# A two-layer convolution and attention kernel: the softmax sum's last step on VectorE, edge and overlap copies on ScalarE, and other places for the first value tiles of an image

## The chip, the core and the metric

The kernel runs on one NeuronCore of one Trainium2 chip. The metric is the device time of one execution in microseconds (us), lower is better. Five engines work side by side, each through its own list of instructions in order: TensorE (PE in the profile), VectorE (DVE), ScalarE (ACT), GpSimd (POOL) and SyncE (SP). SP does no arithmetic here; it issues nearly all DMA transfers.

## What is computed

The input is x, eight images of 256 channels and 64 x 64 pixels in float32. Two layers follow, each as x + layer(groupnorm(x)). Cut to what matters:

```python
# layer 0: per-pixel 3x3 weights made from the image, applied to x3
x1, x2, x3 = conv1x1(x, w1, b1), conv1x1(x, w2, b2), conv1x1(x, w3, b3)   # 32, 32, 256 channels
x2u = unfold3(pad(x2, 1, mode='reflect'))
h = relu(bn1(concat([x1, x2u])));  h = relu(bn2(conv1x1(h, cw1)));  w = conv1x1(h, cw2, cb2)
out = einsum('bgskhw,bgkhw->bgshw', unfold3(zero_pad(x3)), w)

# layer 1: 7x7 local attention with 4 heads, plus a dynamic 3x3 branch
q, k, v = conv1x1(x, Wq) * HD**-0.5, conv1x1(x, Wk), conv1x1(x, Wv)
att = softmax(einsum('bdn,bdkn->bnk', q, unfold7(reflect_pad3(k)) + unfold7(reflect_pad3(pe))))
out_att = einsum('bnk,bdkn->bdn', att, unfold7(reflect_pad3(v)))
wts = softmax(einsum('oc,bchw->bohw', Wfc, x).reshape(b, C, 9, h, w), axis=2)
oc = dwconv(relu(dwconv(x, w1)), w2)                       # depthwise 3x3 twice
out = rate1 * out_att + rate2 * sum(oc * wts, over the 9)
```

## The kernel before, in words

**Bands and steps.** An image is cut into NB = 8 bands of R = 8 rows, so there are 64 bands, written here as (image, band). The main loop goes over the bands g; g starts at -12, and bands below zero are a prologue that does layer 0 alone. In each band the loop makes eight steps s: two halves of the channels (ct = 0, 1; 128 channels each) by four pairs of 8 x 8 pixel tiles (m). Layer 1 of band g runs together with layer 0 of band g + 12, so from (6,4) on there is no layer 0 left to do, and bands get shorter.

**The order is written by hand.** There is no planner. A step is a fixed sequence of calls with six `advance()` calls between them, called places here. `after(n, f)` puts f n places later, and `advance()` runs what is due. `beside(g, s)` returns two lists of calls for a step: `mid` runs in the middle of the step, `end` at its end. What is called first stands first in its engine's list, and an engine that waits holds up all that stands behind it.

**What a step puts on TensorE.** Scores of two tile pairs (`scores`, L737, at even steps, from the keys `kb` and the queries `qb`), the weighted values of the two pairs before (`weighted_values`, L786, from the value tiles `vt`), the transposes of probabilities (L774), two weight maps of the dynamic branch (`branch_weights`, L873), and besides, spread over the steps, queries (L672), keys (L693), values (L592) and the layer-0 matmuls (L328, L369, L430, L466). Results that leave through the PSUM tag `gen` share four buffers, so a matmul into a fifth waits until the oldest has been read.

**Layer 0, small maps.** At step 0 `small_maps` runs L328, and `write_maps` has ScalarE write three shifted copies of x2 and the map x1 into a tile of 10 rows (eight ACTIVATEs, L343 and L347). Then the left and right border columns and the border rows are filled by copies on GpSimd (L351 to L360); a row is also handed to the band before.

**Layer 0, products.** Nine times a band VectorE multiplies a tap weight with shifted x3 (`prod`, L479, two buffers) and GpSimd adds it up (`xg`, L487). x3 comes back from DRAM as `x3q` (L389 to L397).

**Keys.** `queries` makes a new key tile `kb` of 14 rows by 70 columns and copies the six rows that it shares with the band before on GpSimd (L668). `keys` runs L693; its `finish` has VectorE add bias and position (L701) and, for the three reflected columns on either side, do the same again from PSUM (L708, three instructions a piece). In the first and the last band of an image the reflected rows follow on ScalarE (L718), and keys and queries are placed one step earlier.

**Values.** `values` (two halves) computes a band of values, and ScalarE copies it into `vc` (L600; one buffer). `store_values` writes it to a DRAM tile `vd` with its reflected columns (L616 to L625). `value_tile` loads the four tiles `vt` (L642) that the attention reads. An inner band takes 8 loads. The first key band of an image (j = 0) and the last (j = 8) have three mirrored rows; there each mirrored row is loaded by itself, which makes 32 loads. For the next image's first two bands, values are made during band 7 of the current image at steps 4 and 5 (j = 0) and 6 and 7 (j = 1); the tiles of j = 0 are loaded at the end of step 7, those of j = 1 at the ends of steps 0, 1 and 2 of the new image's first band.

**The dynamic branch's softmax.** ScalarE takes the exponentials (L878), GpSimd adds pairs up (L1080). `dynamic_sum` then adds the two halves (L886), adds 1 and limits the sum to 1e37 in one instruction (L889), both on GpSimd; VectorE takes the reciprocal in two halves (L894, placed 9 and 13 places on), and GpSimd multiplies and adds to the result `xr` (L895, L899, L900), which SP stores (L905). For the very last sum of the kernel all of it is on VectorE.

Of the kernel before, what the change touches and what calls it, by code (L numbers as in the profile page):

```python
# [13 lines left out]
ALU = mybir.AluOpType  # L14
# [9 lines left out]
R = 8  # L24
BAND = R * W
NB = H // R
# [21 lines left out]
PAD = KA // 2  # L48
WP = W + 2 * PAD
TQ = 8  # L50
# [3 lines left out]
KW = TQ + 2 * PAD  # L54
# [32 lines left out]
def conv_layers_kernel(ctx: ExitStack, tc: tile.TileContext, ins: dict, out: bass.AP):  # L87
    nc = tc.nc
# [121 lines left out]
    images = [Image() for b in range(B)]  # L210
# [4 lines left out]
    def after(n, f):  # L215
        later.append((place[0] + n, f))
# [118 lines left out]
    def write_maps(b, i, p12):  # L335
        im = images[b]
        t = im.x2[i] = w0.tile([P, HR, W], F32, tag="x2", name=f"x2_{b}_{i}", bufs=2)
        bias = im.bias
        for u in range(2):
            r, o = u * R // 2, 64 * u  # L340
            for q, (dst, src) in enumerate(((1, 0), (0, 0), (0, 1))):
                n = W - (q != 1)
                nc.scalar.activation(  # L343
                    t[32 * q : 32 * q + 32, r + 1 : r + 1 + R // 2, dst : dst + n],
                    p12[o : o + 32, :, src : src + n], AF.Identity, bias=bias[o : o + 32, 0:1],
                )
            nc.scalar.activation(  # L347
                t[96:128, r : r + R // 2, :], p12[o + 32 : o + 64], AF.Identity, bias=bias[o + 32 : o + 64, 0:1]
            )

        nc.gpsimd.tensor_copy(t[0:32, 1 : 1 + R, 0:1], t[0:32, 1 : 1 + R, 2:3])  # L351
        nc.gpsimd.tensor_copy(t[64:96, 1 : 1 + R, W - 1 : W], t[64:96, 1 : 1 + R, W - 3 : W - 2])

        if i == 0:
            nc.gpsimd.tensor_copy(t[0:96, 0, :], t[0:96, 2, :])
        else:
            nc.gpsimd.tensor_copy(t[0:96, 0, :], im.x2[i - 1][0:96, R, :])
            nc.gpsimd.tensor_copy(im.x2[i - 1][0:96, R + 1, :], t[0:96, 1, :])
        if i == NB - 1:
            nc.gpsimd.tensor_copy(t[0:96, R + 1, :], t[0:96, R - 1, :])  # L360

    def value_maps(b, i, mt):

# [200 lines left out]
    def strided(v, at, *dims):  # L564

        return bass.AP(v.tensor, v.offset + at, [v.ap[0], *dims])
# [40 lines left out]
    def store_values(b, j):  # L607
# [9 lines left out]
        for d in range(1, PAD + 1):  # L617
            for to, c in ((PAD - d, d), (PAD + W - 1 + d, W - 1 - d)):
# [3 lines left out]
                else:  # L622
                    for p in range(2):
                        o = vd[at + p : at + p + 2 * count[p] - 1 : 2, to : to + 1].rearrange("u c n -> c u n")
                        nc.sync.dma_start(out=o, in_=vc[p * W + c : p * W + c + 1, : count[p]])  # L625

    def value_tile(b, j, u):


        im = images[b]  # L630
        vd = im.vd[j]
        vt = im.vt[j, u] = w1.tile([CHUNK, 2, C], F32, tag="vt", name=f"vt_{b}_{j}_{u}", bufs=11)
        if j == 0:
            runs = [(PAD, PAD, R - PAD)] + [(PAD - d, PAD + d, 1) for d in range(1, PAD + 1)]
        elif j < NB:
            runs = [(0, 0, R)]
        else:
            runs = [(0, 1, PAD)] + [(PAD - 1 + d, PAD - d, 1) for d in range(1, PAD + 1)]
        for to, at, n in runs:
            for g in range(2):  # L640
                c0 = (2 * u + g) * TQ
                nc.sync.dma_start(  # L642
                    out=vt[to * KW : (to + n) * KW, g], in_=vd[at : at + n, c0 : c0 + KW]
                )

    def new_keys(i):

# [14 lines left out]
    def queries(b, i, ct):  # L662

        im = images[b]
        nm = f"{b}_{i}_{ct}"
        kb = im.kb[i, ct] = w1.tile([P, KW, WP], F32, tag="kb", name=f"kb_{nm}", bufs=3)
        if i:
            nc.gpsimd.tensor_copy(kb[:, : 2 * PAD], im.kb[i - 1, ct][:, R:])  # L668
        qb = im.qb[i, ct] = w1.tile([P, NT, TQ, TQ], F32, tag="qb", name=f"qb_{nm}")
        pq = ps.tile([P, R, W], F32, tag="gen", name=f"pq_{nm}", bufs=4)  # L670
        for kt in range(NCT):
            nc.tensor.matmul(  # L672
                pq, wq[:, kt, ct * P : (ct + 1) * P], im.yp[i][:, kt, PAD : PAD + R],
                start=(kt == 0), stop=(kt == NCT - 1),
            )
        nc.scalar.activation(
            qb.rearrange("p t r c -> p r t c"), pq.rearrange("p r (t c) -> p r t c", c=TQ),
            AF.Identity, bias=bq[:, ct : ct + 1], scale=HD**-0.5,
        )

    def keys(b, i, ct):


        im = images[b]
        first, last = new_keys(i)
        kb, pe = im.kb[i, ct], im.pe[i]
        bk = chan[:, ct, CBK : CBK + 1]
        pieces = []
        for a in range(first, last, R):
            n = min(R, last - a)  # L690
            pk = ps.tile([P, R, W], F32, tag="gen", name=f"pk_{b}_{i}_{ct}_{a}", bufs=4)
            for kt in range(NCT):
                nc.tensor.matmul(  # L693
                    pk[:, :n], wk[:, kt, ct * P : (ct + 1) * P], im.yp[i][:, kt, a : a + n],
                    start=(kt == 0), stop=(kt == NCT - 1),
                )
            pieces.append((a, n, pk))

        def finish():
            for a, n, pk in pieces:  # L700
                nc.vector.scalar_tensor_tensor(  # L701
                    kb[:, a : a + n, PAD : PAD + W], pk[:, :n], bk, pe[:, a - first : a - first + n],
                    ALU.add, ALU.add,
                )

                for d in range(1, PAD + 1):
                    src = (W, n), (W - 1 - 2 * d, 2)
                    nc.vector.scalar_tensor_tensor(  # L708
                        strided(kb, a * WP + PAD - d, (WP, n), (W - 1 + 2 * d, 2)), strided(pk, d, *src), bk,
                        strided(pe, (a - first) * W + d, *src), ALU.add, ALU.add,  # L710
                    )
            if i in (0, NB - 1):
                after(2, reflect)

        def reflect():
            for d in range(1, PAD + 1):
                to, at = (PAD - d, PAD + d) if i == 0 else (last - 1 + d, last - 1 - d)
                nc.scalar.copy(kb[:, to], kb[:, at])  # L718

        return finish  # L720
# [159 lines left out]
    def dynamic_sum(b, i, ct, ex, oc):  # L880

        tot = w1.tile([P, BAND], F32, tag="tots", name=f"tot_{b}_{i}_{ct}", bufs=1)
        xr = images[b].xr[i]

        engine = nc.vector if (b, i, ct) == (B - 1, NB - 1, NCT - 1) else nc.gpsimd
        engine.tensor_add(tot, ex[:, 1], ex[:, 0])  # L886


        engine.tensor_scalar(tot, tot, 1.0, 1.0e37, ALU.add, ALU.min)  # L889
        rec = w1.tile([P, BAND // 2], F32, tag="rec", name=f"rec_{b}_{i}_{ct}", bufs=1)  # L890

# [12 lines left out]
        def store():  # L904
            nc.sync.dma_start(  # L905
                out=out[b].rearrange("(t p) n -> p t n", p=P)[:, :, i * BAND : (i + 1) * BAND], in_=xr
            )

        after(9, lambda: quotient(0))
        after(13, lambda: quotient(1))  # L910
        after(15, weigh)


    def beside(g, s):

        b, i = divmod(g, NB)
        bn, inx = divmod(g + 1, NB)
        mid, end = [], []
# [15 lines left out]

        made = [(b, i + 2, 4)] if g >= 0 and i < NB - 1 else []
        if i == NB - 1 and 0 <= b + 1 < B:
            made = [(b + 1, 0, 4), (b + 1, 1, 6)]
        for bb, j, d in made:
            if s in (d, d + 1) and (j < NB or s == d):
                mid.append(lambda bb=bb, j=j, d=d: values(bb, j, s - d))  # L940
            if s == d + 1:
                end.append(lambda bb=bb, j=j: store_values(bb, j))
            if s == 7 and d == 4:
                for u in range(NT // 2):
                    end.append(lambda bb=bb, j=j, u=u: value_tile(bb, j, u))
        if g >= 0 and i == 0 and s in (0, 1, 2):
            for u in {0: (0,), 1: (1,), 2: (2, 3)}[s]:
                end.append(lambda u=u: value_tile(b, 1, u))

        nxt = [(b, i + 2, 0)] if g >= 0 and i + 2 < NB else []  # L950
        if i == NB - 1 and 0 <= b + 1 < B:
# [25 lines left out]
        if 0 <= g + AHEAD - 2 < B * NB and s in TAPS_AT[g < -1]:  # L977
            u = TAPS_AT[g < -1].index(s)
# [28 lines left out]
    with tc.manual_schedule():  # L1007

        for i, use in enumerate(("xc", "xc", "xr", "xr", "xs", None, None, None)):
            t = None  # L1010
            if use is None:
                t = w1.tile([P, NCT, RP, W], F32, tag="yp", name=f"x_{i}", bufs=3)
                t = t.rearrange("p t r c -> p t (r c)")[:, :, :BAND]
# [15 lines left out]
        for g in range(-AHEAD, B * NB):  # L1029
            b, i = divmod(g, NB)  # L1030
            for s in range(STEPS):
                ct, m = divmod(s, NT // 2)
                mid, end = beside(g, s)
                steer(g, s)
                if g >= 0:
# [17 lines left out]
                    tot = exponentials(nm, prob, nmax)  # L1053
# [128 lines left out]
```

## Time and profile before

| what | value |
|---|---|
| median of 3 runs | 4016.24 us (4015.74 to 4016.27) |
| the profiled execution's own time | 4010.67 us |
| its span in the trace | 4008.9 us |
| mean granted TensorE clock | 0.988 |
| busy share PE, DVE, POOL, ACT | 95%, 85%, 79%, 71% |
| DMA, mean over the span | 117 GB/s |
| loads of value tiles (L642) | 960 |

The page of the profile gives busy times of each engine, groups of instructions by source line, and the chain of work that ended last. The trace answers further views: the timeline of an engine, what an engine's idle time waited for, and busy times in stretches of time. A line of the timeline has the start in us, the busy time, the engine, the source line, the operation, the output and inputs, the shapes and the count; in brackets stands how long the engine sat idle before it and what ended that. A line of the stretches has for each engine its busy us and its number of instructions, then the granted clock and the DMA share. [...]

### The profile page before, as it was taken

To read this page: it belongs to the slowest core of one execution; us is meant where nothing else is said; L and a number is where in the kernel's file an instruction comes from. 1 tells how busy PE (TensorE), PEld (TensorE's weight loads), DVE (VectorE), ACT (ScalarE), POOL (GpSimd) and SP (SyncE) were. 2 spreads that over 40 slices of the span, in tenths; PEclk is the share of its full clock that TensorE was granted. 3 is DMA by queue.
4 is the path that set the end of the run, shared out by engine and by line. 5 is a ranking of instruction groups with operands and counts; after the bars stand their busy time and mean duration, and the time that the engine had idled before them with its cause. 6 is when DMAs were issued, how large, how long until landed. Compare 5 with 4: busy or idle time off the path is not lost.

```text
span 4008.9 us, 72420 instructions
## 1 busy us (share of the span) xinstructions
PE 3807.0 (95%) x24620; PEld 2116.9 (53%) x24620; DVE 3419.8 (85%) x7143; ACT 2839.5 (71%) x6779; POOL 3174.8 (79%) x2156
## 2 busy tenths in 40 slices
PE   6879999999999999999999999999999999999998
PEld 3445555555555555555555555555555555555554
DVE  5868988888888988888988888978988889977888
ACT  3457777677676777777777677777777677676776
POOL 4758988788987988878887888978888888965665
PEclk9989999999999999999999999999999999999999
DMA  8864543544444443444443544444443544322220
GB/s 230 201 165 113 134 114 104 136 125 113 127 115 122 124 124 101 125 132 120 124 115 104 138 125 118 110 130 124 118 115 90 129 116 104 85 61 88 71 65 32
DMA packets 493171, 469.42 MB, mean 117 GB/s; under 512 B 68432, under 2 KB 394624, under 8 KB 492544
## 3 DMA queue, kind: packets, MB, share of 16 engines
q1 hardware_dynamic: 489472, 460.23, 43.4%
q10 hardware_dynamic: 3328, 4.55, 0.3%
q8 instruction: 195, 3.19, 0.3%
q14 instruction: 176, 1.44, 0.1%
HBM read 325.64 MB, written 138.99 MB: 116 GB/s over the span
## 4 chain that ended last, share of the span: by engine, by line
PE 27%; POOL 26%; DVE 22%; ACT 10%; issue 7%; DMA 5%; SPq 3%; POOLq 0%; DVEq 0%; ACTq 0%
PE pf L873 13%; POOL xg L487 13%; POOL ex L1080 6%; DVE prod L479 5%; DVE acc L856 5%; DVE rec L894 4%; PE small L786 3%; ACT x L343 3%; PE sco L737 2%; PE ptp L774 2%; ACT ex L878 2%; DVE prob L751 2%; DMA x3q<-x 2%; PE pq L672 2%; DVE acc L830 2%
## 5 line engine op out<-in xcount | busy, mean ns | idle before, releaser
L873 PE MATMUL pf<-yp,c_wfc 128*128 128x512 f32 x4096 | 1917.1, 597 | 6.2 <-ACT ex L878 5.1
L487 POOL TENSOR_TENSOR xg<-xg,prod 128x1024 f32<-128x1024 f32 x549 | 1200.7, 2187 | 177.2 <-DVE prod L479 148.3
L873 PEld LDWEIGHTS pf<-yp,c_wfc 128*128 128x128 f32 x4096 | 744.0, 191 | 730.3 <-issue 647.1
L1080 POOL TENSOR_TENSOR ex<-ex,ex 128x1024 f32<-128x1024 f32 x384 | 907.9, 2364 | 55.9 <-ACT ex L878 51.8
L479 DVE SCALAR_TENSOR_TENSOR prod<-pw,c_par,x3q 128x1040 f32<-128x1040 f32 x576 | 737.9, 1288 | 124.8 <-PE pw L466 56.1
L830 DVE SCALAR_TENSOR_TENSOR acc<-yp,c_chan,acc 128x504 f32<-128x504 f32 (+3 forms) x1104 | 775.0, 702 | 50.7 <-ACT acc L821 30.3
L856 DVE SCALAR_TENSOR_TENSOR acc<-hid,c_chan,acc 128x504 f32<-128x504 f32 (+3 forms) x1024 | 749.8, 732 | 18.1
L878 ACT ACTIVATE ex<-pf 128x512 f32<-128x512 f32 x1024 | 602.1, 588 | 204.2 <-PE pf L873 184.3
L759 ACT ACTIVATE prob<-prob,nmax 128x196 f32<-128x196 f32 x1024 | 459.2, 451 | 217.1 <-DVE nmax L751 216.9
L768 ACT ACTIVATE prob<-prob,tot 128x196 f32<-128x196 f32 x1024 | 413.0, 452 | 235.3 <-DVE tot L766 235.1
L895 POOL TENSOR_TENSOR tot<-tot,rec 128x256 f32<-128x256 f32 x254 | 185.4, 730 | 412.9 <-DVE rec L894 387.9
L894 DVE RECIPROCAL rec<-tot 128x256 f32<-128x256 f32 x256 | 445.9, 1742 | 17.2 <-POOL tot L889 12.3
L776 ACT COPY pt<-ptp 112x512 f32<-112x512 f32 x511 | 294.8, 577 | 123.4 <-PE ptp L774 122.3
L751 DVE CUSTOM_DVE_ANT_0 prob<-sco,c_mask 128x196 f32<-128x196 f32 x1024 | 324.5, 354 | 20.4 <-PE sco L737 20.2
L786 PE MATMUL small<-pt,vt 112*64 112x64 f32 x8144 | 300.3, 226 | 37.5 <-DMA vt<-vd 37.1
L774 PEld LDWEIGHTS ptp<-ident,prob 128*112 128x112 f32 x2044 | 228.1, 134 | 188.9 <-issue 135.2
L774 PE MATMUL ptp<-ident,prob 128*112 128x128 f32 x2044 | 322.9, 281 | 1.3 <-ACT vc L600 1.3
L786 PEld LDWEIGHTS small<-pt,vt 112*64 112x64 f32 x8144 | 261.5, 138 | 116.7 <-issue 75.4
L737 PE MATMUL sco<-kb,qb 64*64 64x196 f32 x4096 | 236.1, 343 | 39.6 <-DVE kb L708 32.9
L592 PE MATMUL pv<-c_wv,yp 128*128 128x256 f32 (+1 forms) x1056 | 252.8, 382 | 2.6 <-ACT ex L878 2.1
L369 PE MATMUL p<-xc,w3s 128*128 128x512 f32 x512 | 248.4, 609 | 7.0 <-ACT ex L878 7.0
L466 PEld LDWEIGHTS pw<-h2n,c_c 128*128 128x128 f32 x1152 | 173.3, 191 | 153.5 <-issue 113.1
(139 smaller groups left out, 4756.9 us busy)
## 6 DMA issues: line engine op xcount, KB each, us to landing
vt<-vd SPq DMA_DIRECT2D x448, 112.0 KB
x<-x3n SPq DMA_DIRECT2D x128, 264.0 KB
x3q<-x SPq DMA_DIRECT2D x128, 264.0 KB
xc<-in_x SPq DMA_DIRECT2D x64, 512.0 KB
xg<-in_x SPq DMA_DIRECT2D x256, 128.0 KB
x<-xg SPq DMA_DIRECT2D x256, 128.0 KB
yp<-x SPq DMA_DIRECT2D x128, 256.0 KB
xr<-x SPq DMA_DIRECT2D x64, 512.0 KB
```

What stands on the lines that cost most here:

```text
L479: nc.vector.scalar_tensor_tensor(prod[:, :, :RUN], pw[:, j, :RUN].unsqueeze(1).to_broadcast([P, SHARE, RUN]), par[:, PCB2 + k : PCB2 + k + 1],
L487: nc.gpsimd.tensor_add(im.xg[i], im.xg[i], rows(prod))
L759: nc.scalar.activation(prob[:, h, :NKEY], prob[:, h, :NKEY], AF.Exp, bias=nmax[:, h : h + 1], scale=-1.0, accum_out=tot[:, h : h + 1],)
L768: nc.scalar.activation(prob[:, h, :NKEY], prob[:, h, :NKEY], AF.Copy, scale=tot[:, h : h + 1])
L774: nc.tensor.transpose(ptp[:, h, ch], prob[:, h, ch * CHUNK : (ch + 1) * CHUNK], ident)
L786: nc.tensor.matmul(po[half[h], :, t * TQ : (t + 1) * TQ], im.vt[i + ch, m][:n, t, (2 * ct + h) * HD : (2 * ct + h + 1) * HD], pt[:n, h, ch ...
L830: nc.vector.scalar_tensor_tensor(o, yp[:, ct, ra + dr : rb + dr, ca + dc : cb + dc], chan[:, ct, CW1 + k : CW1 + k + 1], o, ALU.mult, ALU.add,
L856: nc.vector.scalar_tensor_tensor(o, hid[:, ra + dr : rb + dr, ca + dc : cb + dc], chan[:, ct, CW2 + k : CW2 + k + 1], o, ALU.mult, ALU.add,)
L873: nc.tensor.matmul(pf, wfc[:, kt, 2 * m + j, ct * P : (ct + 1) * P], images[b].yp[i][:, kt, PAD : PAD + R], start=(kt == 0), stop=(kt == N ...
L878: nc.scalar.activation(ex[:, j].rearrange("p (r c) -> p r c", r=R), pf, AF.Exp)
L894: nc.vector.reciprocal(rec, v)
L1080: after(4, lambda ex=ex, exb=exb: nc.gpsimd.tensor_add(ex, ex, exb))
```

## The change

Four things are edited. (1) In `write_maps` the border copies go from GpSimd to ScalarE, and in `queries` the copy of the overlapping key rows does too. (2) In `keys` the reflected columns are no longer computed on VectorE from PSUM; one place later ScalarE copies them inside the key tile. (3) In `dynamic_sum` the "add 1, limit" instruction moves from GpSimd to VectorE and is placed 7 places later. (4) For j = 0 and j = 8 the mirrored rows are written once in DRAM (`mirror_rows`, three DMAs from `vd` to `vd`, one step after the values were stored), so that every value tile takes 2 loads and a band 8; the next image's first values are made one step earlier (steps 3 and 4, and 5 and 6), and the tiles of j = 1 are loaded in the middle of steps 0 and 2.

```diff
@@ write_maps
-        nc.gpsimd.tensor_copy(t[0:32, 1 : 1 + R, 0:1], t[0:32, 1 : 1 + R, 2:3])
-        nc.gpsimd.tensor_copy(t[64:96, 1 : 1 + R, W - 1 : W], t[64:96, 1 : 1 + R, W - 3 : W - 2])
+        nc.scalar.copy(t[0:32, 1 : 1 + R, 0:1], t[0:32, 1 : 1 + R, 2:3])
+        nc.scalar.copy(t[64:96, 1 : 1 + R, W - 1 : W], t[64:96, 1 : 1 + R, W - 3 : W - 2])
...
-            nc.gpsimd.tensor_copy(t[0:96, 0, :], im.x2[i - 1][0:96, R, :])
-            nc.gpsimd.tensor_copy(im.x2[i - 1][0:96, R + 1, :], t[0:96, 1, :])
+            nc.scalar.copy(t[0:96, 0, :], im.x2[i - 1][0:96, R, :])
+            nc.scalar.copy(im.x2[i - 1][0:96, R + 1, :], t[0:96, 1, :])
...
@@ values
+    def mirror_rows(b, j):
+        vd = images[b].vd[j]
+        for d in range(1, PAD + 1):
+            to, at = (PAD - d, PAD + d) if j == 0 else (PAD + d, PAD - d)
+            nc.sync.dma_start(out=vd[to], in_=vd[at])
@@ value_tile
-        if j == 0:
-            runs = [(PAD, PAD, R - PAD)] + [(PAD - d, PAD + d, 1) for d in range(1, PAD + 1)]
-        elif j < NB:
-            runs = [(0, 0, R)]
-        else:
-            runs = [(0, 1, PAD)] + [(PAD - 1 + d, PAD - d, 1) for d in range(1, PAD + 1)]
-        for to, at, n in runs:
-            for g in range(2):
-                c0 = (2 * u + g) * TQ
-                nc.sync.dma_start(
-                    out=vt[to * KW : (to + n) * KW, g], in_=vd[at : at + n, c0 : c0 + KW]
-                )
+        at, n = (0, R) if j < NB else (1, 2 * PAD)
+        for g in range(2):
+            c0 = (2 * u + g) * TQ
+            nc.sync.dma_start(out=vt[: n * KW, g], in_=vd[at : at + n, c0 : c0 + KW])
@@ queries
-            nc.gpsimd.tensor_copy(kb[:, : 2 * PAD], im.kb[i - 1, ct][:, R:])
+            nc.scalar.copy(kb[:, : 2 * PAD], im.kb[i - 1, ct][:, R:])
@@ keys
-                for d in range(1, PAD + 1):
-                    src = (W, n), (W - 1 - 2 * d, 2)
-                    nc.vector.scalar_tensor_tensor(
-                        strided(kb, a * WP + PAD - d, (WP, n), (W - 1 + 2 * d, 2)), strided(pk, d, *src), bk,
-                        strided(pe, (a - first) * W + d, *src), ALU.add, ALU.add,
-                    )
+            after(1, columns)
...
+        def columns():
+            for a, n, _ in pieces:
+                for d in range(1, PAD + 1):
+                    nc.scalar.copy(
+                        strided(kb, a * WP + PAD - d, (WP, n), (W - 1 + 2 * d, 2)),
+                        strided(kb, a * WP + PAD + d, (WP, n), (W - 1 - 2 * d, 2)),
+                    )
@@ dynamic_sum
-        engine.tensor_scalar(tot, tot, 1.0, 1.0e37, ALU.add, ALU.min)
+        def limit():
+            nc.vector.tensor_scalar(tot, tot, 1.0, 1.0e37, ALU.add, ALU.min)
...
+        after(7, limit)
@@ beside
-            made = [(b + 1, 0, 4), (b + 1, 1, 6)]
+            made = [(b + 1, 0, 3), (b + 1, 1, 5)]
...
+            if s == d + 2 and j in (0, NB):
+                end.append(lambda bb=bb, j=j: mirror_rows(bb, j))
-            if s == 7 and d == 4:
+            if s == 7 and j != 1:
...
-        if g >= 0 and i == 0 and s in (0, 1, 2):
-            for u in {0: (0,), 1: (1,), 2: (2, 3)}[s]:
-                end.append(lambda u=u: value_tile(b, 1, u))
+        if g >= 0 and i == 0 and s in (0, 2):
+            for u in (s, s + 1):
+                mid.append(lambda u=u: value_tile(b, 1, u))
```

More of the change, by code (lines that the diff above doesn't have):

```diff
@@ L349, in write_maps @@
             )
-        nc.gpsimd.tensor_copy(t[0:32, 1 : 1 + R, 0:1], t[0:32, 1 : 1 + R, 2:3])
-        nc.gpsimd.tensor_copy(t[64:96, 1 : 1 + R, W - 1 : W], t[64:96, 1 : 1 + R, W - 3 : W - 2])
+        nc.scalar.copy(t[0:32, 1 : 1 + R, 0:1], t[0:32, 1 : 1 + R, 2:3])
+        nc.scalar.copy(t[64:96, 1 : 1 + R, W - 1 : W], t[64:96, 1 : 1 + R, W - 3 : W - 2])
         if i == 0:
-            nc.gpsimd.tensor_copy(t[0:96, 0, :], t[0:96, 2, :])
+            nc.scalar.copy(t[0:96, 0, :], t[0:96, 2, :])
         else:
-            nc.gpsimd.tensor_copy(t[0:96, 0, :], im.x2[i - 1][0:96, R, :])
-            nc.gpsimd.tensor_copy(im.x2[i - 1][0:96, R + 1, :], t[0:96, 1, :])
+            nc.scalar.copy(t[0:96, 0, :], im.x2[i - 1][0:96, R, :])
+            nc.scalar.copy(im.x2[i - 1][0:96, R + 1, :], t[0:96, 1, :])
         if i == NB - 1:
-            nc.gpsimd.tensor_copy(t[0:96, R + 1, :], t[0:96, R - 1, :])
+            nc.scalar.copy(t[0:96, R + 1, :], t[0:96, R - 1, :])
     def value_maps(b, i, mt):
```

## The prediction

> **What bounds the kernel now.** I read the page first, then TensorE's idle gaps band by band.
>
> ```profile
> PE 3807.0 (95%) x24620; PEld 2116.9 (53%) x24620; DVE 3419.8 (85%) x7143; ACT 2839.5 (71%) x6779; POOL 3174.8 (79%) x2156
> ```
>
> TensorE is the bound nearly everywhere, so an edit is worth only what it does to TensorE's gaps. The stretches of one band each show where they are: (6,0), (6,1), then (7,0), (7,1).
>
> ```profile
> 3147.20:3213.60 66.40, 61.44 (x383) 33.15 (x382) 53.60 (x119) 45.20 (x110) 47.38 (x33) 0.97 0.48 123
> 3213.60:3271.90 58.30, 57.49 (x379) 32.10 (x378) 50.98 (x105) 43.53 (x104) 50.46 (x35) 1.00 0.43 115
> 3597.50:3656.00 58.50, 52.71 (x325) 29.03 (x324) 41.52 (x105) 36.44 (x93) 29.90 (x20) 0.94 0.31 95
> 3656.00:3705.60 49.60, 49.60 (x321) 27.10 (x320) 39.64 (x93) 36.13 (x88) 30.43 (x21) 1.00 0.22 71
> ```
>
> An image's first band takes 8 to 9 us more than the next, though it has only 0.65 us more matmuls (3 more key rows). The timelines of SP, ACT and PE in (6,0) say why:
>
> ```profile
> 3142.50 16.92 SPq L642 DMA_DIRECT2D vt<-vd  x32
> ...
> 3165.55 1.44 SPq L642 DMA_DIRECT2D vt<-vd  x2
> 3167.11 0.40 SPq L553 DMA_DIRECT2D yp<-x  x1
> ```
>
> ```profile
> 3168.50 0.55 PE L786 MATMUL small<-pt,vt 112*64 112x64 f32 x8 [2.08 <-DMA vt<-vd]
> ```
>
> ```profile
> 3171.61 1.13 ACT L562 ACTIVATE yp<-yp,aff 128x896 f32<-128x896 f32 x1 [5.38 <-DMA yp<-x]
> ```
>
> SP needs 16.92 us to issue 32 loads for j = 0. What stands behind them, the tiles of j = 1 and the rows for the next band, comes late, and TensorE and ScalarE wait. Over the run TensorE waits 37.1 us for `vt`.
>
> An ordinary band, (2,2), has only small gaps. TensorE's timeline, ScalarE's and VectorE's:
>
> ```profile
> 1343.16 0.92 PE L737 MATMUL sco<-kb,qb 64*64 64x196 f32 x16 [0.75 <-DVE kb L708]
> ...
> 1354.09 1.98 PE L369 MATMUL p<-xc,w3s 128*128 128x512 f32 x4 [0.18 <-ACT ex L878]
> ...
> 1372.57 0.92 PE L737 MATMUL sco<-kb,qb 64*64 64x196 f32 x16 [0.17 <-DVE kb L708]
> ...
> 1401.55 0.92 PE L737 MATMUL sco<-kb,qb 64*64 64x196 f32 x16 [0.76 <-DVE kb L708]
> ```
>
> ```profile
> 1352.95 0.47 ACT L347 ACTIVATE x<-small,bias 32x256 f32<-32x256 f32 x1
> 1353.44 0.60 ACT L878 ACTIVATE ex<-pf 128x512 f32<-128x512 f32 x1
> ```
>
> ```profile
> 1355.66 0.17 DVE L766 RECIPROCAL tot<-tot 128x2 f32<-128x2 f32 x1 [2.73 <-ACT prob L759]
> ...
> 1389.96 1.30 DVE L479 SCALAR_TENSOR_TENSOR prod<-pw,c_par,x3q 128x1040 f32<-128x1040 f32 x1 [0.53 <-POOL xg L487]
> ...
> 1400.23 0.73 DVE L701 SCALAR_TENSOR_TENSOR kb<-pk,c_chan,pe 128x512 f32<-128x512 f32 x1
> 1400.88 0.52 DVE L708 SCALAR_TENSOR_TENSOR kb<-pk,c_chan,pe 128x16 f32<-128x16 f32 x3
> ```
>
> The three places that stop TensorE (1354.09, 1372.57, 1401.55; call them P1, S4, S0) hang on ScalarE's block of `write_maps` and on VectorE's keys. TensorE has no slack to hide a delay there.
>
> [...] The trace agrees for full partitions (L818, 128x128: 289 ns, the next one 0.19 us later), but L343 and L347 on 32 partitions follow each other at 0.47 us, their full duration. [...] after the 5.78 us gap in (7,0) the granted clock of the band is 0.94.
>
> **The change part by part.**
>
> *Border copies on ScalarE.* Four copies a band (two of 32x8, two of 96x64) stand between L347 at 1352.95 and the exponential at 1353.44, which frees the PSUM buffer that P1 waits for. [...] Taken: 0.7. P1's stall grows from 0.18 to 0.88, and all on ScalarE behind it, L759 of step 1 included, moves by 0.7. GpSimd loses 0.84 us a band.
>
> *Limit on VectorE.* L889 takes 1.92 us on GpSimd; its one run on VectorE took 0.43. It stands after L766 of step 1 (and of step 5), so VectorE's unbroken run from 1355.66 to S4's keys moves by 0.70 + 0.43 = 1.13. It newly waits for GpSimd's L886; that ends at 1349.93 for the first, and for the second, once L889 and the key copy are gone from GpSimd, by my count about 1 us before VectorE gets there. So no wait is added.
>
> *Reflected columns on ScalarE.* L708's 0.44 to 0.52 us leave VectorE; three copies of 128x16 follow on ScalarE[...]. Taken: 0.5. They stand behind L768, which waits for L766.
>
> *Key overlap on ScalarE.* 128x420, [...]twice a band. Behind L768 of steps 2 and 6, where ScalarE next idles 0.80 and 1.04 us for VectorE; cost nothing. [...]
>
> *An ordinary band, summed.* S4: L701 (1371.25 to 1371.98) ends 1.13 later, at 1373.11; L768's pair ends at 1372.08 + 1.13 = 1373.21; columns 0.5; the 0.15 from keys to scores as before: 1373.86 for 1372.57, **+1.29**. That delays the tap weights for which VectorE waits at 1381.43. From there to L701's end VectorE takes 19.53 us; its waits on GpSimd (0.53, and 0.16 before L894) go, since GpSimd is 2.5 us lighter in that stretch; the second limit adds 0.43: 19.27, so L701 ends at 1401.99. L768 ends 0.11 later, columns and hand-over 0.65: 1402.75 for 1401.55, **+1.20 us a band**. There are 33 such bands (bands 1 to 5 of images 0 to 5, and (6,1) to (6,3)): 40 us. Bands (b,6) of six images have S4 alone (the next keys come a step early): 8. Band 7 stalls 1.27 and up to 1.32 us on ScalarE already, after `write_maps` and at step 3; I put 1.9 on each of six: 11. (6,4) and (6,5): 1. From (6,6) on VectorE waits for TensorE: nothing. **Loss 60**; ends 42 (copies overlapped) to 78.
>
> *Value tiles.* 960 loads become 576 and 48 DRAM copies; at a first band SP issues 8 for 32, at 0.53 us each (16.92 / 32) 13 us sooner free. The copies wait for the stores of `vd` and hold SP up, some 2 us by estimate, two steps ahead of the loads; behind them are stores of x1 and a load of x that aren't urgent. In band 7, though, 14 stores (9 us) now precede x3q, which isn't wanted until step 1 of the next band, and ScalarE's next `vc` (one buffer) can wait about 3 us for them; four PSUM buffers cover TensorE. First bands of images 1 to 6 took 66.76, 69.43, 67.16, 68.81, 67.30, 66.36 (405.8). After: 57.3 of matmuls in (6,1) + 0.6 + 1.5 (the 0.79 stall at P1 plus 0.7) + 0.9 and 1.0 (the present ScalarE stalls at steps 4 and 6, grown by the limit) + 1.0 before the next S0 = 62.3, six times 373.8: 32 saved. (7,0): 58.5 to 50.3: 8. (0,0): 72.65, where the first 5.7 us run at half clock: to 65.2: 7.5. Prologue, values one step sooner: 3, between 0 and 8. **Gain 50.5**; ends 35 to 66.
>
> Net +9.5: 4020 for the profiled execution's 4010.67, which lies 5.6 below the median of the runs; **4026 us** on that scale. No change, as far as a measurement here can tell, is within 0.2%, 8 us.
>
> **Rivals.** *Faster (0.28).* The copies overlap[...]: a band grows by 0.9 (30 + 6 + 5 = 41), and the first bands reach 60.0 (gain 66): 3991. For it: L818's 0.19 us. Against: L347's 0.47. It decides below +0.9 us an ordinary band, a length of 59.3. *The limit waits for GpSimd (0.10).* If L886 ends 1 us later than VectorE arrives, all behind it waits, some 1 us in 33 bands: 4060. GpSimd's 5 us idle before L895 speak against. *The gain isn't had (0.12).* One `vc` buffer and the DRAM copies make new waits of image starts, half the gain goes: 4051. For it: ScalarE waited 11.87 us for `vd<-vc` before the first band. *As forecast (0.50)*, 4008 to 4045, of which 0.17 within 0.2%.
>
> **How the numbers follow.** Slower 0.33 + 0.10 + 0.12 = 0.55, same 0.17, faster 0.28. The ends combined give 4016 + 42 - 66 = 3992 and 4016 + 78 - 35 = 4059: range 3990 to 4060. The likeliest case alone: 4008 to 4045.
>
> **What would show it.** Right: band (2,2) at 59.6 us with P1's stall near 0.9, "sco" waiting for ACT in place of DVE; first bands near 62 with no wait on `vt`. Wrong: ordinary bands at 58.4 or below, or first bands above 65.

## The result, and the profile after

The changed kernel takes **4034.73 us** (median of 5 runs, 4029.57 to 4044.25) against 4016.27 for the kernel before (median of 5 runs beside it, 4015.74 to 4021.51): a ratio of 1.0046, 95% interval 1.0031 to 1.0061. It is slower by 18.5 us. The forecast was 4026 with a range of 3990 to 4060, and slower as the likeliest side. The execution profiled took 4035.98 us, its span is 4034.0.

Line numbers have moved by a few in the changed kernel: the scores L737 are here L739, the exponentials L878 are L880, the limit L889 is L892. The page's line of busy times, to be laid beside that of before:

```profile
PE 3802.1 (94%) x24620; PEld 2111.2 (52%) x24620; DVE 3449.8 (86%) x6838; ACT 2974.6 (74%) x7579; POOL 2836.0 (70%) x1661
```

GpSimd lost 339 us of work and ScalarE gained 135. VectorE has 305 instructions fewer and is yet busy 30 us longer, which is a first hint of what the prediction missed.

The stretches of one band each, as the prediction showed them for before: an ordinary band (2,2), then (6,0), (6,1) and (7,0). After the length come busy time and instructions of PE, weight loads, VectorE, ScalarE and GpSimd, then the granted clock.

```profile
1356.00:1416.00 60.00, 57.38 (x378) 31.97 (x378) 53.12 (x103) 45.33 (x116) 45.05 (x27) 1.00 0.47 120
3179.30:3241.20 61.90, 58.92 (x383) 32.42 (x382) 53.10 (x111) 46.51 (x123) 44.60 (x26) 1.00 0.55 140
3241.20:3301.30 60.10, 57.39 (x378) 31.96 (x378) 52.02 (x101) 45.40 (x117) 45.31 (x27) 1.00 0.43 112
3630.80:3681.10 50.30, 50.30 (x325) 27.75 (x324) 40.93 (x98) 37.94 (x104) 25.62 (x18) 1.00 0.34 106
```

Both halves of the forecast are there. The first bands fell from 66.4 to 61.9 and from 58.5 to 50.3 us, and an ordinary band rose from 58.3 to 60.1. SP's timeline in (6,0) has the gain: the mirrored rows are three copies that take SP 1.87 us in all to issue, the loads of `vt` that took 16.92 us for j = 0 alone are now 12 in one row (8 for j = 0 and 4 for j = 1), and the next rows follow directly.

```profile
3171.31 1.87 SPq L632 DMA_DIRECT2D vd<-vd  x3
...
3182.62 8.79 SPq L643 DMA_DIRECT2D vt<-vd  x12
3191.51 0.40 SPq L553 DMA_DIRECT2D yp<-x  x1
```

TensorE's waits for `vt` fell from 37.1 to 1.6 us over the run. What it waits for instead heads the list (engine, line and tile, then who was waited for, us in total, times, longest):

```profile
PE sco L739 <- ACT kb L712: 55.5, 65, 1.9
PE p L369 <- ACT ex L880: 41.4, 39, 1.2
```

In TensorE's timeline of (2,2) the three stalls P1, S4 and S0 have grown. S0 stands at both ends, as the stall ahead of this band and of the next:

```profile
1356.27 0.92 PE L739 MATMUL sco<-kb,qb 64*64 64x196 f32 x16 [1.33 <-ACT kb L712]
...
1368.08 1.98 PE L369 MATMUL p<-xc,w3s 128*128 128x512 f32 x4 [1.06 <-ACT ex L880]
...
1386.76 0.92 PE L739 MATMUL sco<-kb,qb 64*64 64x196 f32 x16 [0.25 <-ACT kb L712]
...
1416.31 0.92 PE L739 MATMUL sco<-kb,qb 64*64 64x196 f32 x16 [1.34 <-ACT kb L712]
```

P1 grew from 0.18 to 1.06. ScalarE's timeline shows the four border copies between the last `write_maps` ACTIVATE and the exponential that P1 waits for; from 1366.56 to 1367.43 is 0.87 us:

```profile
1366.07 0.47 ACT L347 ACTIVATE x<-small,bias 32x256 f32<-32x256 f32 x1
1366.56 0.21 ACT L351 COPY x<-x 32x8 f32<-32x8 f32 x1
1366.79 0.20 ACT L352 COPY x<-x 32x8 f32<-32x8 f32 x1
1367.02 0.24 ACT L357 COPY x<-x 96x64 f32<-96x64 f32 x1
1367.17 0.24 ACT L358 COPY x<-x 96x64 f32<-96x64 f32 x1
1367.43 0.60 ACT L880 ACTIVATE ex<-pf 128x512 f32<-128x512 f32 x1
```

S0 grew from 0.76 to 1.34, and VectorE's timeline has the reason. The first limit of the band takes 0.41 us, the second 1.67, the same instruction on the same shape:

```profile
1369.59 0.41 DVE L892 TENSOR_SCALAR tot<-tot 128x512 f32<-128x512 f32 x1
...
1400.12 1.67 DVE L892 TENSOR_SCALAR tot<-tot 128x512 f32<-128x512 f32 x1
```

No idle time is shown before it: the 1.26 us more stand inside the instruction's own record. GpSimd's timeline at both moments:

```profile
1359.59 1.27 POOL L888 TENSOR_TENSOR tot<-ex 128x512 f32<-128x512 f32 x1
1373.18 0.73 POOL L899 TENSOR_TENSOR tot<-tot,rec 128x256 f32<-128x256 f32 x1 [12.32 <-DVE rec L898]
...
1398.09 1.28 POOL L888 TENSOR_TENSOR tot<-ex 128x512 f32<-128x512 f32 x1
1399.33 4.51 POOL L487 TENSOR_TENSOR xg<-xg,prod 128x1024 f32<-128x1024 f32 x2
```

At 1369.59 GpSimd has nothing to do. At 1400.12 the sum (L888) has been done for 0.75 us, and GpSimd is in the first of two `xg` additions, which ends at 1401.51 (1399.33 and the 2.18 of a single one). The limit ends 0.28 us later. Of the 128 limits, 74 start while GpSimd is idle and take 0.4 us. The other 54 end at the least 0.28 us (median 0.28) after the GpSimd instruction that was running when they started, so most of a limit's own 0.41 us comes after that end; they take 59 us more than 54 times 0.41. The trace shows when the two instructions end; what ties one to the other it doesn't show.

### The profile page after: what moved, and what is told of

The parts are those of the page before. It is cut to its first block, busy times and chain, and to the rows that moved or that the text cites. A ratio compares the mean times of both kernels' runs of the same rounds, so it can differ in the third digit from the quotient of the medians.

```text
span 4034.0 us, 71837 instructions
## 1 busy us (share of the span) xinstructions
PE 3802.1 (94%) x24620; PEld 2111.2 (52%) x24620; DVE 3449.8 (86%) x6838; ACT 2974.6 (74%) x7579; POOL 2836.0 (70%) x1661
## 4 chain that ended last, share of the span: by engine, by line
PE 39%; DVE 36%; ACT 13%; issue 6%; DMA 2%; SPq 2%; POOL 1%; DVEq 0%; POOLq 0%; ACTq 0%
PE pf L875 17%; DVE prod L479 9%; DVE acc L858 8%; DVE rec L898 6%; PE small L788 4%; DVE acc L832 4%; PE pv L592 4%; ACT x L343 4%; PE sco L739 3%; DVE prob L753 3%; PE ptp L776 3%; ACT prob L770 2%; PE pq L671 2%; DVE tot L892 2%; ACT prob L761 2%
## 5 line engine op out<-in xcount | busy, mean ns | idle before, releaser
L479 DVE SCALAR_TENSOR_TENSOR prod<-pw,c_par,x3q 128x1040 f32<-128x1040 f32 x576 | 734.2, 1281 | 119.2 <-PE pw L466 77.7
L832 DVE SCALAR_TENSOR_TENSOR acc<-yp,c_chan,acc 128x504 f32<-128x504 f32 (+3 forms) x1104 | 775.0, 702 | 45.4 <-ACT acc L823 25.1
L880 ACT ACTIVATE ex<-pf 128x512 f32<-128x512 f32 x1024 | 601.9, 588 | 152.9 <-PE pf L875 142.3
L739 PE MATMUL sco<-kb,qb 64*64 64x196 f32 x4096 | 236.3, 344 | 59.6 <-ACT kb L712 55.5
L671 PE MATMUL pq<-yp,c_wq 128*128 128x512 f32 x512 | 244.2, 600 | 21.8 <-ACT ex L880 21.8
L768 DVE RECIPROCAL tot<-tot 128x2 f32<-128x2 f32 x512 | 82.4, 161 | 210.0 <-ACT prob L761 208.3
```

Source lines behind the costliest of these rows:

```text
L479: nc.vector.scalar_tensor_tensor(prod[:, :, :RUN], pw[:, j, :RUN].unsqueeze(1).to_broadcast([P, SHARE, RUN]), par[:, PCB2 + k : PCB2 + k + 1],
L832: nc.vector.scalar_tensor_tensor(o, yp[:, ct, ra + dr : rb + dr, ca + dc : cb + dc], chan[:, ct, CW1 + k : CW1 + k + 1], o, ALU.mult, ALU.add,
L880: nc.scalar.activation(ex[:, j].rearrange("p (r c) -> p r c", r=R), pf, AF.Exp)
```

## The experiments

Times are medians; each group ran beside the kernel before, whose medians were 4013.69, 4013.38, 4014.71 and 4014.91 us. The last two columns are from the traces: the median length of an image's second band, (b,1), for an ordinary one, and of the six first bands (1,0) to (6,0), from the first scores of a band to those of the next.

| kernel | us | ratio to before (95%) | (b,1) | (b,0) |
|---|---|---|---|---|
| before | 4016.27 | 1 | 58.39 | 67.23 |
| the changed kernel | 4034.73 | 1.0046 (1.0031 to 1.0061) | 60.05 | 61.95 |
| dma_only | 3961.35 | 0.9866 (0.9852 to 0.9881) | 58.38 | 61.02 |
| borders_back | 3986.72 | 0.9926 (0.9911 to 0.9941) | 59.30 | 61.05 |
| limit_back | 3976.22 | 0.9907 (0.9891 to 0.9924) | 58.67 | 61.07 |
| limit_two_inputs | 4046.86 | 1.0078 (1.0063 to 1.0093) | 60.56 | 62.20 |
| limit_pointer | 4046.43 | 1.0090 (1.0072 to 1.0107) | 60.59 | 62.20 |
| columns_overlap_back | 4066.03 | 1.0131 (1.0116 to 1.0147) | 60.49 | 62.92 |
| keys_on_scalar | 3935.92 | 0.9808 (0.9793 to 0.9823) | 57.94 | 60.20 |
| dma_early_keys | 4005.44 | 0.9981 (0.9971 to 0.9990) | 58.54 | 60.96 |
| mirror_only | 3960.85 | 0.9868 (0.9853 to 0.9882) | 58.39 | 61.38 |
| places_only | 4041.79 | 1.0068 (1.0051 to 1.0085) | 58.38 | 70.92 |
| overlap_alone | 3940.47 | 0.9818 (0.9803 to 0.9832) | 57.83 | 60.95 |
| mirror_keys | 3933.19 | 0.9801 (0.9784 to 0.9817) | 57.93 | 60.20 |

### dma_only: part (4) alone

The edit is the diff's hunks of `value_tile`, `mirror_rows` and `beside` on the kernel before, and nothing else.

> The kernel before with part (4) of the change alone: mirrored rows written once in DRAM, the next image's first values one step earlier, the tiles of j = 1 in the middle of steps 0 and 2. Theory (the gain is all part 4's, the loss all parts 1 to 3's): ordinary bands stay at 58.4 us, the seven first bands (0,0) to (6,0) take 60 to 62, (7,0) takes 50.3, band 7 takes 63.5 or a little less; the total is 3955 to 3970, some 50 to 60 below before. Rival (part of the gain in the first bands came from a GpSimd relieved by parts 1 to 3): first bands stay at 63 to 65, total above 3975.

It took 3961.35 us, 52 below before, and ordinary bands have the 58.38 us of before. The gain is all part (4)'s and touches only the image starts; what the other three parts do together costs the difference to 4034.73, some 73 us. Band 7 stayed at 63.5.

### borders_back: the border copies on GpSimd again

```diff
-        nc.scalar.copy(t[0:32, 1 : 1 + R, 0:1], t[0:32, 1 : 1 + R, 2:3])
+        nc.gpsimd.tensor_copy(t[0:32, 1 : 1 + R, 0:1], t[0:32, 1 : 1 + R, 2:3])
...
```

> The changed kernel with the border copies of write_maps on GpSimd again. Theory (the copies on ScalarE hold up the exponential that P1 waits for, and all that is behind it): P1's stall falls from 1.06 to about 0.2, an ordinary band from 60.04 to about 59.1, some 40 bands: 37 us less, near 3998. Rival (the delay is taken up again before the next scores): P1's stall falls, but a band by 0.4 or less: 4018 or more.

It took 3986.72 us. TensorE's timeline, a band's P1 and the next S0:

```profile
1347.10 1.98 PE L369 MATMUL p<-xc,w3s 128*128 128x512 f32 x4 [0.18 <-ACT ex L880]
...
1395.43 0.91 PE L739 MATMUL sco<-kb,qb 64*64 64x196 f32 x16 [1.31 <-ACT kb L712]
```

P1 is back at 0.18 and S0 is untouched at 1.31: the band loses 0.75 us, most of the 0.88 that P1 lost. The total falls by 48 where 37 was expected. Of this the bands' sums show 5.2 in ordinary bands (b,1), 5.4 in (b,2) and 3.7 to 8.7 in each of the other kinds, band 7 included (63.59 to 62.72), which the expectation had not counted.

### limit_back: the limit on GpSimd again

```diff
-        def limit():
-            nc.vector.tensor_scalar(tot, tot, 1.0, 1.0e37, ALU.add, ALU.min)
+        engine.tensor_scalar(tot, tot, 1.0, 1.0e37, ALU.add, ALU.min)
...
-        after(7, limit)
```

> The changed kernel with the add and minimum on GpSimd again, straight behind the sum, as before. Theory (the second limit of a band costs VectorE 1.67 us in place of the 0.43 that the prediction took, and that sets S0): the keys at the end of a band come 1.67 us sooner, less 0.5 to 0.7 of waits for GpSimd that return; the first limit's 0.41 goes too; an ordinary band takes 59.0 to 59.3, the total is near 4004. Rival (the time at S0 is the columns' on ScalarE): a band falls by no more than 0.4, total 4020 or more.

It took 3976.22 us, 58 less than the changed kernel, about twice the gain expected. The same two stalls:

```profile
1343.39 1.98 PE L369 MATMUL p<-xc,w3s 128*128 128x512 f32 x4 [1.05 <-ACT ex L880]
...
1390.26 0.92 PE L739 MATMUL sco<-kb,qb 64*64 64x196 f32 x16 [0.32 <-ACT kb L712]
```

Now P1 keeps its 1.05 and S0 falls to 0.32, under the 0.76 of before, though the limit stands on GpSimd as it did there. The price of the two limits is 1.38 us a band. The rest, S0's 0.44 below before, was not in any theory yet and is taken up under overlap_alone.

### limit_two_inputs and limit_pointer: another form for the limit

```diff
-            nc.vector.tensor_scalar(tot, tot, 1.0, 1.0e37, ALU.add, ALU.min)
+            nc.vector.scalar_tensor_tensor(tot, tot, 1.0, cap.to_broadcast([P, BAND]), ALU.add, ALU.min)
```

In limit_pointer the 1.0 is `one`, a column of a constant tile, as well.

> The changed kernel with the limit still on VectorE in its place, but as an instruction with two inputs (add 1, minimum with a constant tile), of the form that the other operations there have. Theory (the limit takes 1.67 us because it waits inside the instruction until GpSimd's running instruction ends, and this form does not): every limit takes 0.7 to 0.75 us, whatever GpSimd does; the second is 0.9 sooner done, the first 0.3 later; an ordinary band takes about 59.4, the total 4010 to 4020. Rival (the extra time is a wait for the sum itself or for a shared memory, whatever the form): the second limit ends again 0.3 us after GpSimd's instruction, at 1.6 us or more, and the total is 4035 or above.

> As limit_two_inputs, but the 1 that is added comes from a column of a tile in place of the instruction's constant, as in L832, of whose 647 instructions that started while GpSimd ran none took over 0.76 us. Theory A (an operation with two inputs from SBUF waits for GpSimd's running instruction where its second input is read again and again from one element, whatever the scalar): the second limit again ends 0.5 us after GpSimd's instruction, at about 1.9 us, total near 4047. Theory B (the constant makes the difference): 0.75 us in every place, an ordinary band takes 59.4, total 4010 to 4020.

Both theories of mine for a form that doesn't wait fell: 4046.86 and 4046.43 us. VectorE's and GpSimd's timelines of limit_two_inputs:

```profile
1400.96 1.94 DVE L894 SCALAR_TENSOR_TENSOR tot<-tot,cap 128x512 f32<-128x512 f32 x1
```

```profile
1400.17 4.77 POOL L489 TENSOR_TENSOR xg<-xg,prod 128x1024 f32<-128x1024 f32 x2
```

Undisturbed this form takes 0.67 us (0.73 with the pointer). Where GpSimd is running it ends 0.55 us (median) after GpSimd's instruction, in 54 cases of 128 again, with either scalar. So the wait is not a matter of the one-input form alone, which undisturbed is the faster (0.41 us for 0.67); this one, with two inputs in SBUF, waits too. (In SBUF lie the kernel's ordinary tiles; PSUM is the memory that its matmuls write to.) Yet L832, in the changed kernel, never takes over 0.76 us in 647 starts while GpSimd runs. My expectations had taken it for the same form, and it isn't: its `acc`, read and written, is a tile of the PSUM pool `ps`, so L832 reads one tensor from SBUF and one from PSUM, while `tot` and `cap` both lie in SBUF. Whether that is what decides was not shown: the limit itself with one input in PSUM was not run. Nor was theory A's reason, the one element read again and again, tried apart from it (`cap` is such an input in both runs), though its number (about 4047) came out.

What GpSimd does next tells the two forms apart. In (0,5) a memset, which writes SBUF and reads nothing, follows the `xg` addition without a gap. First the changed kernel, VectorE and GpSimd, then limit_two_inputs:

```profile
607.36 2.11 DVE L892 TENSOR_SCALAR tot<-tot 128x512 f32<-128x512 f32 x1
606.55 2.17 POOL L487 TENSOR_TENSOR xg<-xg,prod 128x1024 f32<-128x1024 f32 x1
608.65 0.53 POOL L391 MEMSET x3q<- 32x528 f32 x1
```

```profile
607.46 1.90 DVE L894 SCALAR_TENSOR_TENSOR tot<-tot,cap 128x512 f32<-128x512 f32 x1
606.63 2.18 POOL L489 TENSOR_TENSOR xg<-xg,prod 128x1024 f32<-128x1024 f32 x1
608.74 0.54 POOL L393 MEMSET x3q<- 32x528 f32 x1
```

The `tensor_scalar` waits for the memset as well and ends 0.28 us after it; the two-input form ends 0.55 us after the addition and doesn't wait for the memset. It is the same in band 5 of images 0 to 5, the six places where a memset follows so closely.

### columns_overlap_back: reflected columns on VectorE, overlap on GpSimd

```diff
-            nc.scalar.copy(kb[:, : 2 * PAD], im.kb[i - 1, ct][:, R:])
+            nc.gpsimd.tensor_copy(kb[:, : 2 * PAD], im.kb[i - 1, ct][:, R:])
...
-            after(1, columns)
+                for d in range(1, PAD + 1):
...
```

> The changed kernel with the reflected key columns on VectorE again and the overlapping key rows on GpSimd again; border copies and limit stay as changed. Theory (both are neutral: VectorE's 0.44 to 0.52 against 0.45 of ScalarE on the same path, and the overlap hidden on either engine): an ordinary band stays within 0.15 of 60.04, the total within 6 us of the changed kernel's 4034.7. Rival (the columns on ScalarE are part of what made the bands longer): a band falls by 0.4 or more, the total is under 4020.

Wrong, by 31 us: 4066.03. S4 is as it was (0.24), S0 rose from 1.34 to 1.78. VectorE's and GpSimd's timelines ahead of it:

```profile
1406.49 2.14 DVE L889 TENSOR_SCALAR tot<-tot 128x512 f32<-128x512 f32 x1
```

```profile
1404.93 1.28 POOL L885 TENSOR_TENSOR tot<-ex 128x512 f32<-128x512 f32 x1
1406.16 4.51 POOL L487 TENSOR_TENSOR xg<-xg,prod 128x1024 f32<-128x1024 f32 x2
```

GpSimd took the overlap copy (0.54 us) earlier in an unbroken row of work, so it started its `xg` 0.33 us ahead of VectorE's limit where that was 0.79 in the changed kernel, and the limit took 0.47 us longer: here GpSimd's delay of 0.46 us reaches VectorE whole. The run moves two things at once; that the overlap is the one that counts is read from these lines and from overlap_alone below, not from a run of its own. It is 0.45 us in each of the 26 bands (b,1), (b,2), (b,4) and (b,5) of the first images: 12 us. By the sums of the bands the six first bands add some 6, (b,6) some 5, where the S0 behind it is 0.82 for 0.10, and five more stretches at half clock, of which the last section speaks, add 8.

### overlap_alone and keys_on_scalar: what is good for the ordinary band

overlap_alone is dma_only with one line more:

```diff
-            nc.gpsimd.tensor_copy(kb[:, : 2 * PAD], im.kb[i - 1, ct][:, R:])
+            nc.scalar.copy(kb[:, : 2 * PAD], im.kb[i - 1, ct][:, R:])
```

keys_on_scalar has the columns on ScalarE besides, that is, the changed kernel with border copies and limit on GpSimd.

> Part (4), and of the others only the copy of the overlapping key rows on ScalarE; reflected columns on VectorE, border copies and limit on GpSimd. Theory (in keys_on_scalar the copy's 0.54 us on GpSimd made the gain, because VectorE's products waited for GpSimd 0.53 and 0.16 us before S0; the columns are neutral): an ordinary band takes 57.9 to 58.1, S0 0.3 to 0.4, the total is 3933 to 3942. Rival (the columns made the gain): 58.4, S0 at 0.75, total near 3961.

> The changed kernel without its two costly parts: the border copies and the limit are on GpSimd again, the columns and the overlap stay on ScalarE, part (4) stays. Theory (the costs of borders and limit add up, and GpSimd without the overlap no longer holds up VectorE's products as much): P1 falls to 0.18 and S0 to 0.3 or 0.5; an ordinary band takes 57.9 to 58.2, under the 58.4 of before; total 3940 to 3955. Rival (no gain from columns and overlap): 58.4 and 3961, as with part (4) alone.

3940.47 and 3935.92 us, the second a little below its range. overlap_alone has S0 at 0.32 in TensorE's timeline, and in VectorE's a shorter wait for GpSimd:

```profile
1318.30 0.92 PE L736 MATMUL sco<-kb,qb 64*64 64x196 f32 x16 [0.32 <-DVE kb L707]
```

```profile
1364.63 1.30 DVE L479 SCALAR_TENSOR_TENSOR prod<-pw,c_par,x3q 128x1040 f32<-128x1040 f32 x1 [0.41 <-POOL xg L487]
```

Before, that wait was 0.53, and a second of 0.16 stood ahead of L894; the second is gone. A copy of 0.54 us that leaves the row of GpSimd's work ahead of S0 takes 0.55 us off the bands (b,1), (b,2), (b,4) and (b,5), but only 0.08 off (b,3); the kernel is 21 us faster. So GpSimd stands in the loop that sets S0, beside VectorE. The columns are neutral there (57.83 without, 57.94 with), as forecast; by the sums of the bands they bring 4.6 us in the first bands and 3.3 in band 7, which the times of the two kernels (intervals that overlap) can't show by themselves.

### mirror_only and places_only: what part (4) lives on

In mirror_only the rows are mirrored and every tile takes two loads, but steps and places are those of before; in places_only it is the other way round.

> The kernel before with the mirrored rows written once in DRAM and two loads for every value tile; the places of making and loading the first values stay as they were. Theory (the 32 loads on SP were what came late): SP is 11 to 12 us sooner free ahead of (b,0), the waits for the value tiles of j = 1 and for the next rows go, the first bands take 61 to 62 and (7,0) 50.3; the total is 3960 to 3970, nearly all of the 52 us that part (4) brings. Rival (the earlier places bring it): first bands at 64 or more, total above 3985.

> The kernel before with the earlier places alone: first values in steps 3 to 6, tiles of j = 1 in the middle of steps 0 and 2, but still 32 loads for j = 0 and no mirrored rows. Theory (the 32 loads on SP were what came late): SP is still 17 us at the loads ahead of (b,0), though the stores for j = 1 no longer stand behind them; waits for the value tiles stay, first bands take 63 or more, the total is 3985 to 4012. Rival (the earlier places bring it): first bands at 61 to 62, total near 3965.

mirror_only took 3960.85 us, within a microsecond of dma_only: the mirrored rows are all of the gain. places_only is slower than before, 4041.79, and far outside the 3985 to 4012 that I expected. The waits of its TensorE and the row of loads on SP ahead of (6,0) say why:

```profile
PE small L786 <- DMA vt<-vd: 55.5, 10, 11.9
```

```profile
3173.86 16.30 SPq L642 DMA_DIRECT2D vt<-vd  x30
```

Earlier values can't be used earlier while the tiles of j = 0 are loaded at the end of step 7 and hold SP for 16 us and more; the loads of j = 1, now in the middle of step 0, then stand behind all of them, and TensorE waits for `vt` 55.5 us in place of 37.1.

### dma_early_keys: every band's keys a step earlier

```diff
-        early = i in (0, NB - 1)
+        early = True
...
-        early = inx in (0, NB - 1)
+        early = True
```

> Part (4) alone, and besides the keys and queries of every band a step earlier, as only the first and last bands have them. Theory (in an ordinary band TensorE's stalls S0 and S4 are the keys' lateness and nothing else): both go, 0.9 us a band in 33 bands, ordinary bands take 57.5, total near 3932. Rival (the keys then collide with other work of that step, PSUM buffers above all): stalls of the same size stand elsewhere, bands at 58.3 or more, total 3958 or more.

The rival won: 4005.44 us, 44 more than dma_only. S0 and S4 are gone, and in their place TensorE waits for PSUM buffers that ScalarE's exponentials free, as its waits (in total over the run) show:

```profile
PE pf L872 <- ACT ex L877: 40.4, 37, 3.0
PE pq L671 <- ACT ex L877: 31.8, 51, 0.9
```

Of the long ones, 2.6 us stand in (b,3) and 2.1 us in (b,6) of each of the images 0 to 5.

### mirror_keys: the best of the parts

> keys_on_scalar with the places of making and loading the first values as in the kernel before: of the change there remain the mirrored rows, the columns and the overlap. Theory (the earlier places add nothing once the mirrored rows are there, as 3960.9 against 3961.4 without columns and overlap says): within 5 us of keys_on_scalar's 3935.9, band (0,0) 3 to 4 us shorter, the other first bands up to 0.4 longer. Rival (with columns on ScalarE the old places bring waits in band 7): 3945 or more.

3933.19 us, a ratio of 0.9801 (0.9784 to 0.9817), 2.0% below before: the lowest median of the study, though its interval overlaps that of keys_on_scalar. As expected the earlier places add nothing; (0,0) is 4.3 us shorter without them. Of the change this kernel keeps the mirrored rows, the overlap and the columns.

## Why the prediction was right, point by point

**The side and the size.** Slower, 4034.73 for 4026. Part (4) alone brought 52 us where 50.5 was worked out; the other three parts together cost some 73 where it was 60. The spans of the profiled executions differ by 25.1 us where +9.5 was worked out, the medians by 18.5; most of what lies between these two is that the execution profiled before was 5.6 below its median.

**An ordinary band** was put at 59.6 (58.4 + 1.20) and takes 60.04 in (2,2). *Border copies*: 0.7 taken, by my estimate between copies in a row and copies that overlap. In a row they come to 0.9, as an estimate from two other copies of ScalarE in the trace before (L718, 128x70, 248 ns on average; L818, 128x128, 289 ns). 0.87 was measured in ScalarE's timeline, near to that, for the two 32x8 copies follow each other at their full 0.21 to 0.23. *First limit*: 0.43 taken, 0.41 measured. S4 was to come 1.29 later and comes 1.08 later (30.49 us after the band's first scores for 29.41). The 0.16 that I gave the columns isn't there: from L700's start to the scores it is 1.33 us, 1.32 before. *Columns and overlap on ScalarE*: hidden, as taken; three columns' copies take 0.44 to 0.45 us where 0.5 was taken, the overlap's copy 0.53.

**The step that failed is the second limit.** "The second limit adds 0.43" rests on one run of that instruction on VectorE in the trace before, at the very end, where GpSimd had no work. It took 1.67 here, 1.24 more than the sum has. That the band came out only 0.45 longer than forecast is partly luck, for three terms of the sum went the other way. VectorE's row from the tap weights to L700's end takes 20.09 us (1395.62 to 1415.71) where the prediction has 19.27: of the 1.24, 0.42 came back, since with both waits for GpSimd gone the instructions overlap by about 0.08 at their seams, and one product (L479) took 1.20 for 1.30. The tap weights came 0.21 sooner, and the 0.16 of the columns fell away. Over the 33 bands the sum was 40 us and is 48.7: they are not alike, as the sum took them to be, for (b,1) and (b,2) grew by 1.65, (b,5) by 1.8, (b,3) by 1.2 and (b,4) by 0.9. "So no wait is added" was true of semaphores, and was wrong as a statement on time: the wait is inside the instruction. The rival with the limit waiting for GpSimd's sum was not it, for the sum had been done for 0.75 us; but its size, some 1 us a band, was near the 1.24 of the wait that came.

**Bands 6 and 7.** (b,6): 8 forecast, 11.1 measured, of which 3.2 are two stretches at half clock. (b,7): 11 forecast, 4.2 measured, of which 3.4 are two such stretches. The 1.9 a band was mis-sized: it added P1's delay and the limit's. P1's part is there (its stall at `pq` 2.15 for 1.27), the limit's isn't (limit_back has 63.55), and the overlap and columns give 0.9 back (keys_on_scalar 62.63).

**The gain.** First bands of images 1 to 6: 373.8 forecast, 371.7 measured. (7,0): 50.3 forecast, 50.25 measured. (0,0): 65.2 forecast, 67.0 measured. "SP needs 16.92 us to issue 32 loads" was the cause, as mirror_only shows. The 8 loads for j = 0 are issued sooner; that the values are made a step earlier was not needed. The prediction did not count the clock in this gain: before, (1,0) to (6,0) hold eight stretches of 3.41 us at half clock, behind the waits for `vt`, and dma_only has none there. At some 1.6 us each (the price that the last section has) that is about 13 us by estimate. The wait of ScalarE's `vc` came as forecast, about 3.3 us in band 7 of five images for some 0.9 before; it cost TensorE nothing that can be seen, for mirror_only, which has no wait over 1.4 us there in images 0 to 5, takes the same total. So the rival "the gain isn't had" was right that there would be a wait and wrong that it would cost.

**The prologue**, from the first matmul to the first scores of (0,0), was put at 3 us less and is 9.2 longer in this trace (233.7 for 224.6). In the traces of the twelve other kernels it lies between 224.9 and 229.9; limit_two_inputs and limit_pointer, with all three engine parts as changed but for the limit's form, have 229.0 and 228.7. So the parts need not make it 9 us longer. Whether the rest is this execution's own isn't settled, for its time is only 1.25 us above the median of the five runs, which spread over 14.7 us. VectorE there waited 26.3 us for `x3q` from DRAM, 15.9 before.

**The rival "faster"** was to decide below a band of 59.3. Its terms were overlapping copies at the borders and the columns. The borders took 0.87, since of their four copies only the last two overlap (0.15 us from start to start for 0.24 each). The columns did overlap (0.44 to 0.45 for three), but the second limit, which it priced as the forecast did, would have undone it.

## What to carry to other kernels

Price an operation that moves from GpSimd to VectorE beside what GpSimd does at that moment, not by its duration on a quiet chip: the same limit took 0.41 us with GpSimd idle and 1.67 with GpSimd at work, and no wait is listed for it. Look for it as one line with two durations, compare its end with the end of the other engine's instruction, and ask of every input whether it lies in SBUF or in PSUM: the limits that waited had theirs in SBUF, and L832, with one in PSUM, took 0.76 us at most. And undo a change part by part before judging it: here one part brought 52 us, two together cost over 90 (the changed kernel beside keys_on_scalar), and one whose cost was rightly put at nothing, the overlap copy, brought 21 us with the limit on GpSimd, because the engine that it left was in the loop.

## What the runs showed of the hardware that I had not expected

- The VectorE `tensor_scalar` (128x512, float32, SBUF to SBUF), 0.41 us beside an idle GpSimd, ended no sooner than 0.28 us after GpSimd's running instruction in all 54 cases (1.67 us in (2,2), 2.11 in (0,5)); in six of them it outlasted a memset that followed as well, by 0.28 us. The form with two inputs in SBUF was done 0.55 us (median) after GpSimd's instruction, and in the same six places didn't wait for the memset. L832, with one input in SBUF and one in PSUM, showed nothing of the kind in 647 starts (0.76 us at most). What makes the difference was not shown.
- The reverse is small here: in limit_two_inputs the second of the two `xg` additions took 2.51 us for 2.18, with VectorE's limit running 0.47 us into it. In the changed kernel seven memsets (L395) that begin 0.06 us after the addition, with the limit at work, take 0.70 us, where they take 0.53 in limit_two_inputs.
- TensorE's granted clock fell to half after short stalls. The prediction has a slower band, 0.94, with a gap of 5.78 us in it. Here four stretches of 3.41 us at half rate begin after stalls of 1.8 and 2.15 us only, each making the band 1.6 us longer: (1,6) and (4,6) after an S0 of 1.8, (1,7) and (2,7) after the 2.15 at `pq`. The same stalls in the other images had no such stretch, nor had limit_pointer behind its six stalls of 2.14 at `pq`; what makes some count was not settled. The windows of (0,6) and (1,6) side by side, with the granted clock at 1.00 and 0.97:

```profile
623.70:681.60 57.90, 56.02 (x378) 31.43 (x378) 51.52 (x106) 43.77 (x113) 41.44 (x25) 1.00 0.40 100
1109.30:1168.80 59.50, 57.67 (x378) 32.45 (x378) 51.52 (x108) 43.80 (x113) 41.41 (x25) 0.97 0.39 97
```
